# Reordering one pass of a graph layer: where the one-hots of slots 0 and 1, the turn of block A and the request for x stand

## The chip, the core and the metric

The kernel runs on one core of a Trainium2 chip. The engines of the core work side by side, each through its own list of instructions in order, and wait for one another by semaphores: TensorE (PE, with its weight loads shown as PEld), VectorE (DVE), ScalarE (ACT), GpSimd (POOL) and SyncE (SP), which here only issues transfers. The metric is the device time of one execution in microseconds; lower is better. The time before the change is 260.56 us, the median of three runs from 260.49 to 260.68 us.

## The reference

There are 12500 nodes with 128 numbers each (x) and 412500 directed edges with 48 numbers each, sorted by their receiver `dst`. What is computed is

```
h   = relu(layernorm(x))                       # per node, 128 numbers
agg = segment_sum(edge_attr_48, dst, 12500)    # per node, the sum of its edges' 48 numbers
u   = graph_globals[0]                         # one row for all nodes
out = x + relu([h, agg, u] @ W1 + b1) @ W2 + b2
```

W1 has 256 columns and W2 has 128. All is float32.

## The kernel before

**Tiling.** Edges come in chunks of 768; four chunks make a group, eleven groups make one pass. There are 12 passes, each over 33792 edges and 1024 nodes, and an epilogue for the rest (212 nodes). The 1024 nodes of a pass are two blocks of 512, A and B; each block has four pieces of 128 nodes. The eleven groups sit in six slots: slots 0 to 3 hold two groups each, slot 4 holds one (group 5), slot 5 holds groups 10 and 11.

**Sums over edges.** For each slot DVE builds one-hot matrices that say to which of 28 neighbouring receivers an edge belongs (`onehots`, L745, tile `oh`), PE multiplies them with the edges (`sums`, L801, into one of two PSUM banks `s`), and ACT copies the result out (L805, tile `ss`). A second set of small one-hot matrices (`places`, L751, and `places_near`, `places_far`, L764) then puts these sums at their node (`place`, L823, and `place_ends`, L785, into banks `ax` and `ay`). `place_ends` comes after all `place` and needs slot 5's copy, here called ss5, from its second matmul on.

**The nodes.** DVE takes statistics of x (`stats`, L831), a few small instructions make the variance (`variance`, L836 to L841), ACT takes the root (`root`, L845), DVE makes scale and shift (`shift`, L850 and L851), ACT normalises and applies relu piece by piece (`norm`, L857, tiles `xna` and `xnb`). PE turns the pieces (`turn`, L866), ACT copies the turned block out (L867, `hta` and `htb`), `sums_out` (L872) copies the edge sums, and the first layer is `layer_x` (L876) and `layer_e` (L881), ended by relu on ACT (L886, `hida` and `hidb`).

**The second layer runs one pass late.** `second` (L907) multiplies the hidden numbers of the pass before with W2, sixteen matmuls for block A; then DVE adds it to x + b2 and keeps it (L911, `holda`, `holdb`). For block B, three of four pieces are done early (`second_begun`, L901) and the last one later. After it DVE forms the next x + b2 (`add_b`, L861, `xba`, `xbb`), and only then may the next x be asked for: `load_x` (L597), issued by ACT for both blocks. The edge loads of L597 are issued by SP, each as soon as the sums of its slot have been taken.

**Order.** `body` writes all operations of one pass in one list; an engine's own order is the order of the list, cut down to that engine. `Flow.order` finds the waits from what each operation reads and writes. DVE, ACT and SP run the list in a hardware loop. PE runs it in blocks joined by branches: the list is cut at the operation named in `f.mark`, and the part behind the mark runs at the head of the loop. In the first pass there is no hidden layer to multiply yet, so the operations named in `f.brief` are passed over by a branch (from L301 on).

In the list of `body` before, what matters stands so: slots 0 and 1 are summed, then statistics of A, `farthest` (L692, L694), `fetch` (L730, which reads the receivers for the one-hots of the next pass), slot 2, statistics of B, variance, root, one-hots of slot 0, slot 3, shift, one piece of A normalised, slot 4, two pieces, one-hots of slot 1, slot 5, one piece, then all of B.

Of the kernel before, what the change touches and what calls it, by code (L numbers as in the profile page):

```python
# [28 lines left out]
R = 4  # L29
# [25 lines left out]
class Flow:  # L55
# [14 lines left out]
    def op(self, eng, name, reads, writes, emit, dma=False, late=None):  # L70
        self.seq.append(dict(eng=eng, name=name, r=tuple(reads), w=tuple(writes), emit=emit, dma=dma, it=self.at, late=late or {}))
# [119 lines left out]
    def run(self):  # L191
# [22 lines left out]
        def ahead(e, late=False):  # L214
            for n, c in sorted(self.ahead[e].items()):
                if (e == "PE" and n in self.weights) == late:
                    self.of[e].wait_ge(self.sem[n], (self.rank[n, c] + self.extra[n]) * self.unit(n))

        def repeat(o, i):
            waits = []  # L220
            for n, back in self.body.get(o["name"], []):
                u = self.unit(n)
                waits.append((n, self.sem[n], regs[(o["eng"], u, (self.at_lo[n] - lo - back + self.extra[n]) * u)]))
            self.emit(o, waits, i)
# [26 lines left out]
        pe = nc.tensor  # L251
        blocks = {}

        def part(name, over, come=True):

            if come:
                pe.br("pe_" + name)
            blocks[name] = nc.switch_bb("pe_" + name, parent=over and blocks[over])

        def either(under, yes, no):  # L260

            pe.br_lt(j, under, on_true="pe_" + yes, on_false="pe_" + no)

        n = 4
# [35 lines left out]
        at = "first"  # L300
        for brief, some in groupby(own[:cut], lambda o: o["name"] in self.brief):  # L301
            some = list(some)
            if not brief:
                for o in some:
                    if o["name"] in self.stops:
                        stop = "at_" + o["name"]
                        at = "go_" + o["name"]
                        above, under, to = over[stop]
                        part(stop, above)
                        either(under, to, at)  # L310
                        part(at, stop, False)
                    repeat(o, None)
                continue
            either(n + 1, "brief", "whole")
            part("brief", at, False)
            ahead("PE", True)
            for o in some:
                if o["name"] in self.sem:
                    pe.sem_inc(self.sem[o["name"]], 1)
            pe.br("pe_both")  # L320
            part("whole", at, False)
            for o in some:
                repeat(o, None)
            part("both", at)
        pe.br("pe_head")
        part("after", "gate2", False)
        self.straight(end)
# [151 lines left out]
def kernel(  # L479
# [37 lines left out]
    def bank(name):  # L517
        return psum.tile([P, BN], F32, name=name)
# [4 lines left out]
    ph = [bank("ph0"), bank("ph1")]  # L523
# [66 lines left out]
    f = Flow(nc, tc)  # L590
    op = f.op
    A, B, Z = 0, 1, 2
# [128 lines left out]
    def fetch(j):  # L721

        it = (f.at or 0) + j
        g0, g1 = it * GI + 1, min(NG, (it + 1) * GI + 1)
        m = GI * CG
        blocks = [b for b in range(NB) if b * P < g1 * CG and (b + 1) * P > g0 * CG]
        rv = rel_i.rearrange("p g (c t) -> p (g c) t", t=T)
        at = lambda i: ((i + j) * GI + 1) * CG

        op("DVE", "fr", ["relz"] + [f"rel{b}.{t0}" for b in blocks for t0 in (0, 3)], ["rel_i"], lambda i: [nc.vector.tensor_scalar(  # L730
            rv, (rel[:, :, at(i):at(i) + m] if isinstance(i, int) else rel[:, :, ds(at(i), m)]).rearrange("p t c -> p c t"),
            0.0, None, OP.add)])
# [20 lines left out]
    def onehots(s):  # L753
        g = SLOTS[s]
        onehot(s, oh[s], ["rel_i"], rel_i[:, g[0] - 1:g[0]] if len(g) == 1 else rel_i[:, g[0] - 1:g[1]:g[1] - g[0]])
# [32 lines left out]
    def keep_ends():  # L788
        op("ACT", "ssf", ["ss5"], ["ssf"], lambda i: [nc.scalar.copy(ssf, ss[5])])
# [43 lines left out]
    def variance(n, ks, m=P):  # L833
        s, v = sm[n][:m], st[n][:m]
        op("DVE", f"sm{n}.0", [f"st{k}" for k in ks], [f"sm{n}a"], lambda i: [
            nc.vector.tensor_tensor(s[:, 0:2], v[:, :, 1:3].rearrange("p r c -> p c r"), v[:, :, 4:6].rearrange("p r c -> p c r"), OP.add)])  # L836
        op("DVE", f"sm{n}.1", [f"st{k}" for k in ks], [f"sm{n}b"], lambda i: [
            nc.vector.tensor_tensor(s[:, 2], v[:, :, 1], v[:, :, 4], OP.subtract)])
        f.chain("DVE", f"sm{n}.2", [f"sm{n}a"], [f"sm{n}b"],
            lambda: nc.vector.tensor_tensor(s[:, 2], s[:, 2], s[:, 2], OP.mult),  # L840
            lambda: nc.vector.scalar_tensor_tensor(s[:, 3], s[:, 2], D / 4.0, s[:, 1], OP.mult, OP.add))  # L841

    def root(n, m=P):
        op("ACT", f"sq{n}", [f"sm{n}b", "eps"], [f"sc{n}"], lambda i: [
            nc.scalar.activation(sc[n][:m], sm[n][:m, 3], AF.Sqrt, bias=eps[:m], scale=1.0 / D)])  # L845
# [7 lines left out]
    def norm(k, some, m=P):  # L853
        n, c = k // 2, k % 2 * R
        for r in some:
            op("ACT", f"xn{k}.{r}", [f"x{k}", f"x{k}t", f"sc{n}", f"sh{n}"], [f"xn{k}"], lambda i, r=r: [
                nc.scalar.activation(xn[k][:m, r], xt[k][:m, r], AF.Relu, bias=sh[n][:m, c + r:c + r + 1], scale=sc[n][:m, c + r:c + r + 1])])  # L857
# [5 lines left out]
    def turn(k, m=P, bk=None, key="PT", eng="ACT"):  # L863
        pv = (pt if bk is None else bk)[:, :RR[k] * P].rearrange("p (r c) -> p r c", r=RR[k])
        copy = nc.scalar.copy if eng == "ACT" else nc.vector.tensor_copy
        op("PE", f"tu{k}", [f"xn{k}", "ident"], [key], lambda i: [nc.tensor.transpose(pv[:, r, :m], xn[k][:m, r], ident[:m, :m]) for r in range(RR[k])])  # L866
        op(eng, f"hT{k}", [key], [f"hT{k}"], lambda i: [copy(hT[k][:, :, :m], pv[:, :, :m])])  # L867

    def sums_out(k, m=P):
        h, r = HI * (k % 2), RR[k]  # L870
        op("ACT", f"ag{k}", [f"bk{k % 2}"], [f"ag{k}"], lambda i: [
            nc.scalar.copy(ag[k // 2][h:h + DE, :, :m], agg[k % 2][h:h + DE, :m * r].rearrange("p (c r) -> p r c", r=r))])  # L872
# [25 lines left out]
    def second_begun(k, bk, key, n):  # L898
        ov = bk.rearrange("p (r d) -> p r d", r=R)
        op("PE", f"w2{k}a", [f"hid{k}.{a}" for a in range(NH)] + ["w2"], [key], lambda i: [  # L900
            nc.tensor.matmul(ov[:, r], hid[k][:, a, r], w2[:, a], start=(a == 0), stop=(a == NH - 1)) for r in range(n) for a in range(NH)])  # L901
# [101 lines left out]
    def body(it):  # L1003
        f.at = it

        def add_slots(*some):
            for s in some:
                sums(s)
                if it < NIT - 1:
                    load_e(s, 1)  # L1010

        keep = lambda i: (i + NIT - 2) % (NIT - 1)
        add_slots(0, 1)
        stats(A)
        farthest()
        fetch(1)
        add_slots(2)
        stats(B)
        variance(0, (A, B))
        root(0)  # L1020
        onehots(0)
        add_slots(3)
        shift(0)
        norm(A, (0,))
        add_slots(4)
        norm(A, (1, 2))
        onehots(1)
        add_slots(5)
        norm(A, (3,))
        norm(B, range(R))  # L1030
        onehots(2)
        onehots(3)
        place(0, (0, 1))
        for s in (1, 2, 3, 4):
            place(s)
        place_ends((0, 1))
        second(A, P, ph[A], "PH0", keep)
        add_b(A)
        for s in (4, 5):
            onehots(s)  # L1040
        second_begun(B, ph[B], "PH1", R - 1)
        sums_out(A)
        sums_out(B)
        if it < NIT - 1:
            load_x(A, lambda i: (i + 1) % NIT * IN)
        turn(A)
        turn(B, P, po, "PO")
        second(B, P, ph[B], "PH1", keep, R - 1)
        add_b(B)
        keep_ends()  # L1050
        if it < NIT - 1:
            load_x(B, lambda i: (i + 1) % NIT * IN + BN)
        places_far()
        fetch_off(1)
        for s in (0, 1, 2, 3, 4):
            places(s)
        places_near()
        layers(layer_x)
        layers(layer_e)
        layers(relu)  # L1060
# [51 lines left out]
    f.at = NIT + 1  # L1112
    ends = [f"ot{k}" for k in range(3)] + [f"x{k}" for k in (A, B)] + [f"hold{k}.{j}" for k in (A, B) for j in range(NIT - 1)]
    op("SP", "end", [], ends, lambda i: [nc.sync.nop(nofuse=True)])
    f.mark, f.half, f.stops = "tu0", "of2", ("su1.b", "su1.c", "su2.b")
    f.brief, f.weights = ("w20", "w21a"), ("lw1h", "lw1a", "lw1b", "lw2")
    f.order((0, NIT - 1))
    tc.mark_branch_hint_location("skip", engines=[ET.PE, ET.DVE])
# [35 lines left out]
```

## Time and profile before

| what | us |
|---|---|
| median of three runs | 260.56 |
| the profiled execution, its own time | 260.67 |
| its span, first to last instruction | 258.9 |
| PE busy in the span | 238.8 |
| DVE busy | 230.8 |
| ACT busy | 127.9 |
| mean length of one pass, from pass 1 to pass 11 (second layer of A to second layer of A) | 18.07 |

The span is cut into 40 slices on the page of the profile; there the transfers are busy in almost every slice, and so are PE and DVE. With three resources nearly full, the share of busy time doesn't say which of them sets the pace. For that one has to follow, in the timeline of one pass, which instruction waits for which other, around the pass and back to the same instruction of the next one. The pass from 116.5 to 134.6 us is used for this below; times of it are counted from the start of the span.

A timeline row has the start, the duration, the engine, the line, the operation and the tiles; instructions of one form that follow each other are merged into one row with their count, and such a row's duration goes to the end of the last one. Where the engine stood idle before it, brackets say for how long and what released it.

### The profile page before, as it was taken

Reading aid. Unit: us, or ns where it says so; the run is one execution under the profiler, and the core shown is the slowest. Engines: PE = TensorE matmul, PEld = TensorE weight load, DVE = VectorE, ACT = ScalarE, POOL = GpSimd, SP = SyncE. Lnnn points to the kernel's source line nnn. Section 1 sums busy time; section 2 is a strip of 40 time slices with the busy share of each in tenths; the row PEclk is TensorE's granted clock in tenths of the full one; section 3 lists DMA queues with packets and bytes.
Section 4 is the critical chain, followed back from the end, with each engine's and each line's share of the span. In section 5 each row is a group of like instructions: output and inputs, shape, how many; then the busy total and the mean of one; then the engine's idle time right before and its main releaser. Section 6 shows DMA issues by size and latency. Waiting matters only on the chain.

```text
span 258.9 us, 17101 instructions
## 1 busy us (share of the span) xinstructions
PE 238.8 (92%) x7539; PEld 188.7 (73%) x7540; DVE 230.8 (89%) x572; ACT 127.9 (49%) x315; POOL 5.2 (2%) x18
## 2 busy tenths in 40 slices
PE   1866699899999999999999999999999999999990
PEld 1766565885976968949949869779589499598680
DVE  6699998978998998998998989989989989989740
ACT  5510273553644725725835646447257358355520
POOL 5000000000000000000000000000000000002000
PEclk9967579999999999999999999999999999999999
DMA  6999999999999999999999999999999999969951
GB/s 189 339 385 388 364 387 392 390 390 393 377 392 389 389 392 387 390 392 384 390 394 385 390 393 386 392 386 385 391 383 390 391 389 390 394 230 363 366 208 65
DMA packets 79508, 94.33 MB, mean 364 GB/s; under 512 B 3227, under 2 KB 72797, under 8 KB 79494
## 3 DMA queue, kind: packets, MB, share of 16 engines
q1 hardware_dynamic: 76086, 88.06, 95.5%
q10 hardware_dynamic: 3312, 6.03, 6.1%
q8 instruction: 7, 0.11, 0.2%
q0 software_dynamic: 96, 0.07, 0.1%
q14 instruction: 7, 0.06, 0.1%
HBM read 87.75 MB, written 6.40 MB: 364 GB/s over the span
## 4 chain that ended last, share of the span: by engine, by line
PE 78%; SPq 14%; DMA 4%; issue 1%; DVE 0%
PE s L801 23%; SPq L597 14%; PE ph L907 12%; PE ph L876 7%; PE ax L823 6%; PE ph L901 6%; PE pt L881 4%; PE pt L876 4%; DMA e<-in_edge_attr_dram 4%; PE ph L881 4%; PE po L876 4%; PE pt L866 2%; PE po L866 2%; PE ax L785 1%; PE ay L785 1%
## 5 line engine op out<-in xcount | busy, mean ns | idle before, releaser
L745 DVE TENSOR_TENSOR oh<-iota_v,rel_i 128x1344 f32<-128x1344 f32 (+1 forms) x78 | 108.7, 1435 | 0.0
L801 PEld LDWEIGHTS s<-e,oh 128*28 128x28 f32 x6336 | 74.2, 111 | 16.8 <-issue 14.5
L801 PE MATMUL s<-e,oh 128*28 128x48 f32 x6336 | 76.9, 212 | 7.4 <-issue 3.5
L886 ACT ACTIVATE hida<-pt,bias 128x512 f32<-128x512 f32 x12 | 8.2, 687 | 50.2 <-PE pt L881 50.2
L857 ACT ACTIVATE xna<-xa,shab,scab 128x128 f32<-128x128 f32 x48 | 23.7, 493 | 13.0 <-DVE shab L851 12.6
L805 ACT COPY ss<-s 128x96 f32<-128x96 f32 (+1 forms) x72 | 16.5, 229 | 26.5 <-PE s L801 25.7
L751 DVE TENSOR_SCALAR pl<-iota_w,off_i 128x186 f32<-128x186 f32 x117 | 27.6, 311 | 0.4
L907 PE MATMUL ph<-w,hida 128*128 128x128 f32 x192 | 24.6, 281 | 0.0
L857 ACT ACTIVATE xnb<-xb,shab,scab 128x128 f32<-128x128 f32 x48 | 23.5, 490 | 1.2
L907 PEld LDWEIGHTS ph<-w,hida 128*128 128x128 f32 x192 | 22.3, 191 | 0.6
L823 PE MATMUL ay<-pl,ss 128*48 128x186 f32 (+1 forms) x120 | 20.9, 324 | 0.0
L823 PE MATMUL ax<-pl,ss 128*48 128x186 f32 (+1 forms) x120 | 20.9, 324 | 0.0
L823 PEld LDWEIGHTS ax<-pl,ss 128*48 128x48 f32 x120 | 14.5, 129 | 4.1
L831 DVE BATCH_NORM_STATS2 stab<-xb 128x6 f32<-128x128 f32 x48 | 10.5, 282 | 6.9 <-DMA xb<-in_x_dram 6.9
L901 PE MATMUL ph<-w,hidb 128*128 128x128 f32 x132 | 16.5, 275 | 0.0
L901 PEld LDWEIGHTS ph<-w,hidb 128*128 128x128 f32 x132 | 15.6, 192 | 0.0
L823 PEld LDWEIGHTS ay<-pl,ss 128*48 128x48 f32 x120 | 14.5, 129 | 0.0
L876 PE MATMUL pt<-hta,w1h 128*128 128x512 f32 x24 | 13.5, 643 | 0.4 <-ACT hta L867 0.4
L881 PE MATMUL po<-ags,w1a 48*128 48x512 f32 x24 | 13.5, 641 | 0.0
L881 PE MATMUL pt<-ags,w1a 48*128 48x512 f32 x24 | 13.5, 641 | 0.0
L867 ACT COPY hta<-pt 128x512 f32<-128x512 f32 x12 | 7.0, 586 | 12.2 <-PE pt L866 12.2
L881 PE MATMUL ph<-ags,w1a 48*128 48x512 f32 x48 | 12.3, 589 | 0.0
(151 smaller groups left out, 330.3 us busy)
## 6 DMA issues: line engine op xcount, KB each, us to landing
e<-in_edge_attr_dram SPq DMA_DIRECT2D x133, 576.0 KB, 8.7
xa<-in_x_dram ACTq DMA_DIRECT2D x11, 256.0 KB, 5.4
xb<-in_x_dram ACTq DMA_DIRECT2D x11, 256.0 KB, 5.4
out_dram<-holda SPq DMA_DIRECT2D x11, 256.0 KB, 3.1
out_dram<-holdb SPq DMA_DIRECT2D x11, 256.0 KB, 3.1
holda<-in_dst_dram SPq DMA_DIRECT2D x4, 384.0 KB, 5.6
e<-in_edge_attr_dram SPq DMA_DIRECT2D x1, 720.0 KB, 4.7
xa<-in_x_dram SPq DMA_DIRECT2D x1, 256.0 KB, 6.6
```

The source lines that it names most:

```text
L597: return [f.of[eng].dma_start(dst_ap(i) if callable(dst_ap) else dst_ap, src_ap(i) if callable(src_ap) else src_ap)]
L745: op("DVE", f"oh{name}", reads + ["iota_v"], [f"oh{name}"], lambda i: [nc.vector.tensor_tensor(ov, iota_v[:, None, None, :].to_broadcast([ ...
L751: nc.vector.tensor_scalar(out[:, j], iota_w, o[j], None, OP.is_equal) for j in range(len(o))])
L801: nc.tensor.matmul(S[k][NV * c:NV * c + V, j * DE:(j + 1) * DE], o[:, (j * CG + c) * T + t], ev[:, j * CG + c, t * DE:(t + 1) * DE], start ...
L805: op("ACT", f"ss{name}", [f"S{k}"], [f"ss{name}"], lambda i: [nc.scalar.copy(sv.rearrange("p j d -> p (j d)"), S[k][:, :m * DE])])
L823: out.append(nc.tensor.matmul(agg[bk][h:h + DE, at:at + w], sv[:, j], pv[:, j, frm:frm + w], start=bk in fresh and bk not in seen, stop=Tr ...
L831: op("DVE", f"st{k}", [f"x{k}", f"x{k}t"], [f"st{k}"], lambda i: [nc.vector.bn_stats(st[k // 2][:m, c + r], xt[k][:m, r]) for r in range(R ...
L857: nc.scalar.activation(xn[k][:m, r], xt[k][:m, r], AF.Relu, bias=sh[n][:m, c + r:c + r + 1], scale=sc[n][:m, c + r:c + r + 1])])
L876: nc.tensor.matmul(o, w1h[:, a * P:(a + 1) * P], hT[k][:, :, :m], start=first, stop=False, skip_group_check=True)])
L881: nc.tensor.matmul(o, w1a[h:h + DE, a * P:(a + 1) * P], ag[k // 2][h:h + DE, :, :m], start=False, stop=True, skip_group_check=True)])
L901: nc.tensor.matmul(ov[:, r], hid[k][:, a, r], w2[:, a], start=(a == 0), stop=(a == NH - 1)) for r in range(n) for a in range(NH)])
L907: nc.tensor.matmul(ov[:m, r], hid[k][:, a, r, :m], w2[:, a], start=(a == 0), stop=(a == NH - 1)) for r in range(begun, RR[k]) for a in ran ...
```

## The change

```diff
@@ the PE list with brief operations
-            either(n + 1, "brief", "whole")
-            part("brief", at, False)
-            ahead("PE", True)
+            tag = some[0]["name"]
+            either(n + 1, "brief_" + tag, "whole_" + tag)
+            part("brief_" + tag, at, False)
+            if tag == self.brief[0]:
+                ahead("PE", True)
             for o in some:
                 if o["name"] in self.sem:
                     pe.sem_inc(self.sem[o["name"]], 1)
-            pe.br("pe_both")
-            part("whole", at, False)
+            pe.br("pe_both_" + tag)
+            part("whole_" + tag, at, False)
             for o in some:
                 repeat(o, None)
-            part("both", at)
+            part("both_" + tag, at)
+            at = "both_" + tag
@@ body
         stats(A)
         farthest()
         fetch(1)
+        onehots(0)
         add_slots(2)
         stats(B)
         variance(0, (A, B))
+        onehots(1)
+        add_slots(3)
         root(0)
-        onehots(0)
-        add_slots(3)
         shift(0)
-        norm(A, (0,))
         add_slots(4)
-        norm(A, (1, 2))
-        onehots(1)
+        norm(A, (0, 1))
         add_slots(5)
-        norm(A, (3,))
+        norm(A, (2, 3))
         norm(B, range(R))
         onehots(2)
         onehots(3)
@@ body, after place_ends, second(A), add_b(A) and the one-hots of slots 4 and 5
-        second_begun(B, ph[B], "PH1", R - 1)
         sums_out(A)
         sums_out(B)
+        turn(A)
+        second_begun(B, ph[B], "PH1", R - 1)
         if it < NIT - 1:
             load_x(A, lambda i: (i + 1) % NIT * IN)
-        turn(A)
         turn(B, P, po, "PO")
@@ the mark
-    f.mark, f.half, f.stops = "tu0", "of2", ("su1.b", "su1.c", "su2.b")
+    f.mark, f.half, f.stops = "tu1", "of2", ("su1.b", "su1.c", "su2.b")
```

On DVE the one-hots of slot 0 move from behind the variance to behind `fetch`, ahead of the statistics of B, and those of slot 1 from behind the shift to ahead of it. On ACT the root moves behind the copy of slot 3, two pieces of A (not three) are normalised ahead of slot 5's copy and two (not one) behind it, the copy of slot 4 comes ahead of all of them, and the copy of the turned A comes ahead of the request for A's next x. On PE, A is turned right behind its second layer and ahead of the begun second layer of B. The two second layers are then no longer neighbours in PE's list, so each gets its own branch, and the cut of the list moves to the turn of B. No operation is added or left out.

## The prediction

> **What bounds the kernel now.** I read the page first, then the waits of DVE, then the chain that ended last, then one pass in the timeline, engine by engine.
>
> ```profile
> span 258.9 us, 17101 instructions
> DMA  6999999999999999999999999999999999969951
> GB/s 189 339 385 388 364 387 392 390 390 393 377 392 389 389 392 387 390 392 384 390 394 385 390 393 386 392 386 385 391 383 390 391 389 390 394 230 363 366 208 65
> PE 78%; SPq 14%; DMA 4%; issue 1%; DVE 0%
> ```
>
> The transfers are busy throughout, at 384 to 394 GB/s in most slices, yet the chain of the end runs over PE for 78%. Its pieces in order of time say where PE begins to set the end:
>
> ```profile
> 39.59 10.01 DMA e<-in_edge_attr_dram
> 49.65 0.71 PE s L801 x48
> 52.24 1.98 PE ph L907 x16
> ...
> 232.90 1.98 PE ph L907 x16
> ```
>
> Until 49.65 us edges are late (passes 0 and 1). From the second layer of A in pass 1 to that in pass 11 the chain is PE's: 232.90 - 52.24 = 180.66 us for ten passes, **18.07 us a pass**. A full PE could be the bound itself, or be paced by something that it waits for a little in each pass. DVE's waits name the candidate:
>
> ```profile
> DVE stab L831 <- DMA xb<-in_x_dram: 6.9, 11, 0.8
> DVE holda L911 <- PE ph L907: 1.6, 1, 1.6
> ```
>
> DVE waits once a pass, about 0.63 us (6.9 / 11), for B's x; for PE's second layer it waited in one pass only. DVE's own pass:
>
> ```profile
> 116.48 0.87 DVE L831 BATCH_NORM_STATS2 stab<-xa 128x6 f32<-128x128 f32 x4
> ...
> 117.87 0.41 DVE L730 TENSOR_SCALAR rel_i<-rel 128x264 f32 x1
> 118.90 0.87 DVE L831 BATCH_NORM_STATS2 stab<-xb 128x6 f32<-128x128 f32 x4 [0.62 <-DMA xb<-in_x_dram]
> ...
> 120.39 1.55 DVE L745 TENSOR_TENSOR oh<-iota_v,rel_i 128x1344 f32<-128x1344 f32 x1
> 121.86 0.19 DVE L850 RECIPROCAL scab<-scab 128x8 f32<-128x8 f32 x1
> 122.09 0.17 DVE L851 SCALAR_TENSOR_TENSOR shab<-smab,scab 128x8 f32<-128x8 f32 x1
> 122.17 4.49 DVE L745 TENSOR_TENSOR oh<-iota_v,rel_i 128x1344 f32<-128x1344 f32 x3
> 126.58 0.68 DVE L911 TENSOR_TENSOR holda<-ph,xba 128x512 f32 x1
> 127.30 0.69 DVE L861 TENSOR_TENSOR xba<-xa,b_sb 128x512 f32<-128x512 f32 x1
> ...
> 130.86 0.69 DVE L861 TENSOR_TENSOR xbb<-xb,b_sb 128x512 f32<-128x512 f32 x1
> ...
> 134.55 0.86 DVE L831 BATCH_NORM_STATS2 stab<-xa 128x6 f32<-128x128 f32 x4
> ```
>
> Nothing but those 0.62 us is idle here: 134.55 - 116.48 = 18.07 us, 17.45 of work and the wait. The wait closes a loop: xbb ends at 131.55, only then is the next xb asked for, and it lands late:
>
> ```profile
> xa<-in_x_dram ACTq DMA_DIRECT2D x11, 256.0 KB, 5.4
> xb<-in_x_dram ACTq DMA_DIRECT2D x11, 256.0 KB, 5.4
> ```
>
> 131.55 + 5.4 = 136.95, 18.05 after 118.90. So xb's loop sets the pace. But there is a **second loop of the same length**, from DVE's shift over ACT and PE back to DVE:
>
> ```profile
> 121.00 0.24 ACT L805 COPY ss<-s 128x96 f32<-128x96 f32 x1 [0.19 <-PE s L801]
> ...
> 122.29 0.49 ACT L857 ACTIVATE xna<-xa,shab,scab 128x128 f32<-128x128 f32 x1 [1.05 <-DVE shab L851]
> 122.69 0.18 ACT L805 COPY ss<-s 128x48 f32<-128x48 f32 x1
> 122.82 1.02 ACT L857 ACTIVATE xna<-xa,shab,scab 128x128 f32<-128x128 f32 x2
> 123.74 0.22 ACT L805 COPY ss<-s 128x96 f32<-128x96 f32 x1
> 123.87 0.49 ACT L857 ACTIVATE xna<-xa,shab,scab 128x128 f32<-128x128 f32 x1
> ...
> 126.24 0.56 ACT L872 COPY ags<-ax 48x512 f32<-48x512 f32 x1
> 126.81 0.58 ACT L872 COPY ags<-ay 48x512 f32<-48x512 f32 x1
> 128.02 0.34 ACTq L597 DMA_DIRECT2D xa<-in_x_dram  x1
> 128.41 0.59 ACT L867 COPY hta<-pt 128x512 f32<-128x512 f32 x1 [1.01 <-PE pt L866]
> ```
>
> ```profile
> 123.90 0.28 PE L785 MATMUL ax<-plf,ssf 128*48 128x140 f32 x1
> 124.02 0.32 PE L785 MATMUL ay<-pln,ss 128*48 128x140 f32 x1
> ...
> 124.47 2.05 PE L907 MATMUL ph<-w,hida 128*128 128x128 f32 x16
> ```
>
> The shift ends at 122.26 (122.09 + 0.17). ACT normalises three pieces of A ahead of the copy of slot 5 (123.74 to 123.96). place_ends needs that copy from its second matmul on, which starts 0.06 behind it, at 124.02. The second layer of A follows at 124.47 and ends at 126.52; holda starts at 126.58. DVE came to holda at that same moment, behind the one-hots, so no wait is shown, but the room is 0.06 us at most.
>
> **The change part by part.**
>
> *Slot 0's one-hots ahead of B's statistics.* They fill the place of the wait: xbb still ends 4.97 behind holda's start (131.55 - 126.58), so xb lands 4.97 + 5.4 = 10.4 behind it. The statistics of B now come 7.97 (134.55 - 126.58) + 1.80 (116.48 to fetch's end at 118.28) + 0.04 + 1.47 = 11.28 behind holda. **-0.62 us** for xb's loop; 0.9 us of room, and if an x load grew by more than that the wait would be back. 1.47 is the place of one one-hot (120.39 to 121.86, also 4.41 / 3 from 122.17 to 126.58). The 0.04 is the step between two DVE instructions of which the second needs the first (reciprocal's end 122.05 to 122.09): the one-hots now stand right behind fetch, whose result they read.
>
> The Trainium skill, "VectorE: DVE Perf Modes", section "The DRAIN you can't avoid", says that a DVE instruction doesn't start before the pipeline of the one ahead has emptied, and that a semaphore between them cost nothing extra. By that the 0.04 is nothing, 0.4 us less in ten passes. The rows differ both ways: unlinked one-hots start 1.47 apart though each takes 1.55, linked ones leave 0.04.
>
> *Slot 1's one-hots ahead of the shift.* On DVE they only change places, 1.47 us either way, but the shift and all of ACT's normalisation now stand behind them. They do cover the root (before, slot 0's did that). From holda to the shift's end, before: 7.97 + 1.80 + 0.62 + 1.49 (118.90 to 120.39, statistics and variance) + 1.47 + 0.40 = 13.75. After: 7.97 + 1.80 + 0.04 + 1.47 + 1.49 + 1.47 + 0.40 = 14.64. **+0.89 us.** The root behind slot 3's copy costs nothing: that copy starts 4.5 us into DVE's pass (121.00 - 116.48), the shift then 6.3 into it (1.80 + 0.04 + 1.47 + 1.49 + 1.47), and the root takes 0.3.
>
> *Two pieces, not three, ahead of slot 5's copy.* From the shift's end to the copy's start, before 123.74 - 122.26 = 1.48; after, 0.03 to the first piece and 0.92 for two (122.82 to 123.74) = 0.95. **-0.53 us.** The copy of slot 4 moves out of the way for nothing, between root and shift.
>
> *The rest of that loop* stays: copy to second layer 0.73 (123.74 to 124.47), second layer to holda 2.11 (124.47 to 126.58). Sum before: 13.75 + 1.48 + 0.73 + 2.11 = **18.07**, the pass measured. After: 14.64 + 0.95 + 0.73 + 2.11 = **18.43**. DVE's own work would take it to holda 0.9 us earlier (17.45 + 0.04 = 17.49 us a pass), but there it now waits for the second layer, which waits for ss5, which waits for the shift. What goes as a wait for xb comes back, larger, as a wait for PE.
>
> *A turned early, its copy ahead of asking for xa.* In the row above, A's copy starts 0.04 behind the request (128.02 + 0.34), which had waited for xba (127.99). Now it can't be held there. But behind ss5 there is one piece more (about 0.5), so sums_out starts 3.0 behind ss5's start instead of 2.50, the two copies take 1.14, and hta is copied from 4.2 to 4.8 behind ss5 instead of 4.67 to 5.26. A gain of some 0.5 in hta, of which PE can use little (its first layer starts at 129.04, 0.04 behind the end of hta, and about when the four matmuls ahead of it were through), and on a stretch that now ends in a wait for ss5: **nothing**. The request for xa follows at 4.7 instead of 4.28 behind ss5 and lands 5.4 later, 10.1; A's next statistics come at 2.84 + 7.97 = 10.8. It is hidden by 0.7 us; without that cover DVE would wait for xa. SP's queue of edge loads isn't passed by anything.
>
> *The second branch on PE.*
>
> ```profile
> 126.36 1.50 PE L901 MATMUL ph<-w,hidb 128*128 128x128 f32 x12
> ...
> 127.70 0.60 PE L866 MATMUL pt<-ident,xna 128*128 128x128 f32 x4
> ...
> 129.04 1.13 PE L876 MATMUL pt<-hta,w1h 128*128 128x512 f32 x2
> ```
>
> No row prices it alone. Bounds: nothing, since the cut of the list, with the loop's own branches, lies between the first two of these rows, and the turn starts before the twelve matmuls end (127.86); and 0.45 us, the whole stretch from place_ends' gated matmul to the second layer, which has a branch already. I take nothing, from the nearer rows; the new branch also lies behind the second layer of A, outside the loop of 18.43.
>
> **The sum.** +0.36 us a pass, ten passes behind pass 1's second layer: +3.6 us. Passes 0 and 1 wait for edges, and the epilogue behind 232.90 is the same list. The profiled execution took 260.67 us, 0.11 above the median of 260.56: 264.3 by the one, **264.2 us** on the scale of the median.
>
> **The rivals.**
>
> *Faster: the change does what it seems meant to.* The place is holda. If DVE, running ahead, doesn't meet the second layer of A there, because slot 5's copy is made as soon as slot 5 is summed and not behind two pieces, the loop of 18.43 is open. Then PE binds, whose only gaps in the rows above are 0.12 ahead of the gated matmul and less for hta: about 17.9 us a pass. The transfers allow hardly more: eleven edge loads of 576 KB and two of 256 KB are 7.01 MB a pass, at the 394 GB/s of the best slice 17.8 us. At 17.95 ten passes give back 1.2 us: 259.4. It decides from the point where the shift ends 0.36 us earlier than I reckon. For it: the wait that is removed is the only one DVE has in each pass. Against it: ACT works in order, and the copy stands behind the pieces in the list. Chance 0.08.
>
> *Same: one of the two loops has more room than one pass shows*, and +0.36 shrinks below 0.05 a pass. Against it: the second sum before hits 18.07 exactly. 260.1 to 261.1; chance 0.05.
>
> *Slower still: the loop of 18.43 and something more*, xa landing behind A's statistics, or the new branch exposed. Another 0.1 to 0.2 a pass would give 265.2 to 266.2. Chance 0.12.
>
> *Much slower: PE's new wait lowers its clock.*
>
> ```profile
> PEclk9967579999999999999999999999999999999999
> ```
>
> In the third to sixth slices, where PE waits for edges, the granted clock falls to between 0.5 and 0.7. Were half a microsecond a pass enough for that, a second layer, the turns and the first layer (some 10 us of PE a pass) could take up to twice as long, 100 us more. Against it: the clock holds at 0.9 or more over all passes that have PE's small gaps, and PE would still be busy for 97% of a pass. Chance 0.01.
>
> The Trainium skill, "TensorE: Matmul & The Clock Gate", section "Part 1: The HAM clock gate (the \"warmup\" mystery)", puts the idle time after which the clock is halved at about 3.4 us. By that rule this case falls away.
>
> **How the numbers follow.** The forecast has 0.74. Its terms are read to 0.01 us, about ten of them, and ten passes multiply an error: 0.1 a pass is 1 us, 263.2 to 265.2. To take in part of the slower case the range goes to 265.4, and down to 262.6 for a loop shorter by 0.16. A measurement of this kernel tells about 0.2% (0.5 us) from no change. Faster 0.08, within 0.2% 0.05, slower 0.87.
>
> **What the changed profile would show.** If right: DVE's wait for xb is gone (6.9 us to under 1), and a new one of holda for PE's L907 stands at about 0.9 us a pass, 9 us in ten; the second layers of A lie 18.4 apart; ss5 starts 0.95 behind the shift's end; place_ends shows a gap of about half a microsecond ahead of its second matmul; hta waits for nothing; the rate falls to about 381 GB/s; SP waits longer for PE. If holda shows no wait and the pass is below 18.0, the loop is wrong. If the pass is above 18.5, the branch or xa is the place to look.

## The result, and the profile after

The changed kernel took 264.2 us (median of four runs, 263.59 to 264.65) against 260.62 us before (four runs, 260.49 to 261.26): **1.3% slower**, ratio 1.0131, 95% interval 1.0102 to 1.016. The profiled execution took 263.89 us, 3.2 us more than the one before (260.67). One execution of all, of the version below with the root moved alone, took 399.3 us at a granted clock of 0.579 and is left out of that version's ratio.

From the page of the changed kernel, the span, the rate of the transfers in 40 slices, and the chain that ended last by engine:

```profile
span 262.0 us, 17127 instructions
GB/s 199 346 389 386 363 387 392 391 390 386 389 392 389 390 392 376 385 392 369 390 394 362 390 380 372 392 372 386 392 363 388 392 365 390 394 189 373 365 186 64
DVE 50%; PE 18%; SPq 14%; issue 7%; ACT 4%; DMA 4%; DVEq 1%
```

The chain has moved from PE (78%) to DVE (50%), and from the sixteenth slice on the rate dips to 362 to 380 in every second or third slice, where before it held 383 to 394. Its pieces in order of time (start, duration, what) give the length of a pass:

```profile
51.89 2.00 PE ph L910 x16
...
236.05 1.98 PE ph L910 x16
```

(236.05 - 51.89) / 10 = **18.42 us a pass** against 18.07. Ten passes cost 3.5 us more; pass 1 happened to begin its second layer 0.35 us earlier (51.89, not 52.24), and 3.15 remain. DVE's waits (what waited for what, us in total, times, longest):

```profile
DVE holda L914 <- PE ph L910: 9.8, 11, 1.4
...
DVE stab L834 <- DMA xa<-in_x_dram: 0.5, 1, 0.5
```

The wait for xb, 6.9 us in 11 passes, isn't in the list any more. In its place holda waits 9.8 us for the second layer. One pass of DVE in the timeline of the changed kernel:

```profile
117.12 0.86 DVE L834 BATCH_NORM_STATS2 stab<-xa 128x6 f32<-128x128 f32 x4
...
118.51 0.41 DVE L733 TENSOR_SCALAR rel_i<-rel 128x264 f32 x1
118.95 1.56 DVE L748 TENSOR_TENSOR oh<-iota_v,rel_i 128x1344 f32<-128x1344 f32 x1
120.43 0.86 DVE L834 BATCH_NORM_STATS2 stab<-xb 128x6 f32<-128x128 f32 x4
...
121.92 1.55 DVE L748 TENSOR_TENSOR oh<-iota_v,rel_i 128x1344 f32<-128x1344 f32 x1
123.39 0.20 DVE L853 RECIPROCAL scab<-scab 128x8 f32<-128x8 f32 x1
123.62 0.17 DVE L854 SCALAR_TENSOR_TENSOR shab<-smab,scab 128x8 f32<-128x8 f32 x1
...
127.57 0.69 DVE L914 TENSOR_TENSOR holda<-ph,xba 128x512 f32 x1 [0.84 <-PE ph L910]
...
135.54 0.87 DVE L834 BATCH_NORM_STATS2 stab<-xa 128x6 f32<-128x128 f32 x4
```

ACT and PE in the same pass:

```profile
122.25 0.18 ACT L808 COPY ss<-s 128x48 f32<-128x48 f32 x1
123.83 1.02 ACT L860 ACTIVATE xna<-xa,shab,scab 128x128 f32<-128x128 f32 x2 [1.40 <-DVE shab L854]
124.75 0.22 ACT L808 COPY ss<-s 128x96 f32<-128x96 f32 x1
...
128.94 0.59 ACT L870 COPY hta<-pt 128x512 f32<-128x512 f32 x1
129.01 0.35 ACTq L600 DMA_DIRECT2D xa<-in_x_dram  x1
```

```profile
124.37 0.40 PE L788 MATMUL ax<-plf,ssf 128*48 128x140 f32 x2
125.02 0.32 PE L788 MATMUL ay<-pln,ss 128*48 128x140 f32 x1 [0.25 <-ACT ss L808]
...
125.48 2.05 PE L910 MATMUL ph<-w,hida 128*128 128x128 f32 x16
```

Read it backwards from holda. It starts at 127.57, when the second layer (125.48) is through. That layer stands behind place_ends, whose gated matmul starts 0.65 us behind the first (124.37 to 125.02; 0.12 before the change): PE waits for slot 5's copy. The copy starts at 124.75, behind two pieces of A, and these behind the shift, which ends at 123.79 and not earlier because slot 1's one-hots stand ahead of it. DVE then stands still 0.84 us.

### The profile page after: what moved, and what is told of

The parts are those of the page before. It is cut to its first block, busy times and chain, and to the rows that moved or that the text cites. A ratio compares the mean times of both kernels' runs of the same rounds, so it can differ in the third digit from the quotient of the medians.

```text
span 262.0 us, 17127 instructions
## 1 busy us (share of the span) xinstructions
PE 241.2 (92%) x7539; PEld 189.1 (72%) x7540; DVE 231.8 (88%) x572; ACT 129.7 (50%) x315; POOL 5.0 (2%) x18
## 4 chain that ended last, share of the span: by engine, by line
DVE 50%; PE 18%; SPq 14%; issue 7%; ACT 4%; DMA 4%; DVEq 1%
DVE oh L748 20%; SPq L600 14%; PE ph L910 10%; DVE pl L754 7%; DVE stab L834 6%; DMA e<-in_edge_attr_dram 4%; ACT xna L860 4%; DVE holda L914 3%; DVE holdb L914 2%; PE ay L788 2%; DVE plf L767 2%; DVE rel_i L733 2%; DVE pln L767 1%; DVE far L695 1%; DVE smab L839 1%
## 5 line engine op out<-in xcount | busy, mean ns | idle before, releaser
L914 DVE TENSOR_TENSOR holda<-ph,xba 128x512 f32 x12 | 8.3, 691 | 9.8 <-PE ph L910 9.8
L879 PE MATMUL pt<-hta,w1h 128*128 128x512 f32 x24 | 12.4, 598 | 0.0
L879 PE MATMUL po<-htb,w1h 128*128 128x512 f32 x24 | 12.3, 592 | 0.0
```

Of the source, the lines that this page charges most:

```text
L879: nc.tensor.matmul(o, w1h[:, a * P:(a + 1) * P], hT[k][:, :, :m], start=first, stop=False, skip_group_check=True)])
L914: op("DVE", f"ho{k}", [key, f"xb{k}"] + (["spare"] if k == A else []), [f"hold{k}.{keep(f.at)}"], lambda i: [nc.vector.tensor_tensor(cols( ...
```

## The experiments

**The theory.** The pass is set by the loop holda, DVE up to the shift, pieces of A, slot 5's copy (ss5), second layer of A, holda. **Rival 1**: all normalising is late, so the turn and the first layer are; how many pieces stand ahead of ss5 is no matter. **Rival 2**: the second branch and the early turn cost PE.

| kernel | us (median) | ratio to before, 95% interval | us a pass |
|---|---|---|---|
| no piece of A ahead of ss5 | 259.63 | 0.9947 (0.9923 to 0.9972) | 17.93 |
| one piece | 259.59 | 0.9948 (0.9931 to 0.9965) | 17.94 |
| two pieces (the changed kernel) | 264.2 | 1.0131 (1.0102 to 1.016) | 18.42 |
| three pieces | 269.51 | 1.0326 (1.0261 to 1.0392) | 18.94 |
| moves of the one-hots without the turn | 264.47 | 1.0138 (1.0073 to 1.0202) | 18.41 |
| the turn alone | 261.24 | 1.0025 (0.9997 to 1.0053) | 18.07 |
| slot 0's move without slot 1's | 259.5 | 0.9955 (0.9939 to 0.9972) | 17.94 |
| slot 1's without slot 0's | 269.29 | 1.0331 (1.0308 to 1.0354) | 18.94 |
| before, slot 0's one-hots moved | 264.57 | 1.0156 (1.0116 to 1.0196) | 18.49 |
| before, the root moved | 260.44 | 0.9982 (0.9964 to 1.0) | 18.05 |
| before, both of these moved | 259.36 | 0.9938 (0.9913 to 0.9962) | 17.94 |
| no piece, slot 4 not loaded anew | 269.18 | 1.0328 (1.0305 to 1.0351) | 17.91 |
| no piece, a quarter of slot 4 loaded | 258.92 | 0.9931 (0.9906 to 0.9955) | 17.90 |

A pass is the distance of the second layers of A in pass 1 and pass 11 on the chain, divided by ten.

### Pieces ahead of slot 5's copy: none, one, three

Three edits of the changed kernel, in one cut:

```diff
         add_slots(4)
-        norm(A, (0, 1))
+        # none: nothing    one: norm(A, (0,))    three: norm(A, (0, 1, 2))
         add_slots(5)
-        norm(A, (2, 3))
+        # none: norm(A, range(R))    one: norm(A, (1, 2, 3))    three: norm(A, (3,))
```

> As the changed kernel, but no piece of A is normalised ahead of slot 5's copy (all four behind it). Theory (the loop shift, two pieces, slot 5's copy, second layer of A, holda sets the pass of 18.42 us): the copy no longer waits for the shift, that loop is open, holda hardly waits; the next bound is some 17.95 us a pass (transfers, and the way over the turned A to the first layer, which I work out as 14.64 + 5.85 + 5.51 + 7.74 + 2.11 = 35.85 us for two passes). Ten passes at -0.47: about 259.5 us, faster than both kernels. Rival 1 (the loss is that all normalising comes later, so turn and first layer are late): the number of pieces ahead of the copy does not matter, 264.2 or, since one copy stands ahead of them, 264 to 265. Rival 2 (the second branch and the early turn cost PE): 264.2.

> As the changed kernel, but three pieces of A ahead of slot 5's copy, as before the change. Theory: 0.53 us more from the shift's end to that copy, pass 18.42 + 0.53 = 18.95 us, ten passes +5.3: 269.5 us, and holda's wait for PE grows from 0.9 to about 1.4 us a pass. Rival 1 and rival 2: 264.2, since neither the shift nor the branches move.

> As the changed kernel, but one piece of A ahead of slot 5's copy. Theory: the loop is 14.64 + 0.43 + 0.73 + 2.11 = 17.91 us, just under the 17.93 us that the pass took with no piece ahead, so that one binds: 259.6 us, 259.2 to 260.0. With none 17.93, one 17.93, two 18.42, three 18.94 the line has its bend between one and two pieces. Rival (each piece ahead costs its half a microsecond from none on): 262.

DVE's waits, first with none, then with three:

```profile
DVE holda L914 <- PE ph L910: 4.3, 11, 0.7
```

```profile
DVE holda L914 <- PE ph L910: 16.0, 11, 2.3
```

Neither the one-hots nor the branches move here, and the time goes from 259.6 over 264.2 to 269.5 us, with the bend between one and two pieces where the sum puts it (0.43 instead of 0.95 from shift to copy). From two to three pieces a pass grows by 0.52, one piece on ACT. Both rivals fall as the cause: with none and with three pieces they had 264.2, at most 265. holda still waits 0.4 us a pass with none (4.3 / 11): there DVE is ahead of PE and nothing behind it is late.

### The turn, and the moves of the one-hots, each alone

```diff
-        sums_out(A)
-        sums_out(B)
-        turn(A)
         second_begun(B, ph[B], "PH1", R - 1)
+        sums_out(A)
+        sums_out(B)
         if it < NIT - 1:
             load_x(A, lambda i: (i + 1) % NIT * IN)
+        turn(A)
...
-    f.mark, f.half, f.stops = "tu1", ...
+    f.mark, f.half, f.stops = "tu0", ...
```

> The moves of the one-hots with the order on ACT up to the second layer of A; the turn of A, its copy and the request for x stand as before the change, and the two second layers are neighbours again with one branch. Theory: nothing of the turn lies on the loop: 264.2 us, 263.9 to 264.6, pass 18.42. Rival 2 (branch and early turn cost PE): 259.5 to 260.6.

The kernel with the turn alone keeps the lines with a minus and has the one-hots, root and pieces of the kernel before.

> The kernel before with only the early turn of A, its copy ahead of the request for x, and the second branch. Theory: the loops of 18.07 us stay, xb's wait of some 0.6 us a pass stays: 260.6 us, within 0.3 of before. Were the 0.05 to 0.1 us that PE waits for hta worth something: 259.6 to 260. Rival 2: 263 to 264.2.

The moves of the one-hots, with the order on ACT that goes with them, bring the whole loss without the turn, 18.41 us a pass. The turn alone leaves the pass at 18.07 and xb's wait in place (7.0 us in 11 passes). Its ratio has 1 within the interval: no gain, and no cost that these ten runs could tell.

### Slot 0's move and slot 1's, each without the other

```diff
 without slot 1's:                     without slot 0's:
         variance(0, (A, B))                    fetch(1)
-        onehots(1)                    -        onehots(0)
         add_slots(3)                           add_slots(2)
...                                    ...
         norm(A, (0, 1))                        variance(0, (A, B))
+        onehots(1)                    +        onehots(0)
         add_slots(5)                           onehots(1)
```

> As the changed kernel, but slot 1's one-hots again behind the shift and slot 5's copy on the list; two pieces of A stay ahead of that copy. Theory: from holda to the shift's end 14.64 - 1.47 = 13.17 us and some 0.45 us of waiting for the root, which nothing covers now; loop 13.6 + 0.95 + 0.73 + 2.11 = 17.4 us, open; DVE's own pass 17.49 + 0.45 = 17.94 and the transfers' 17.93 bind: 259.6 us, 259.2 to 260.0, DVE waiting for ACT's root 0.4 to 0.5 us a pass instead of for xb or PE. Rival (the whole reordering, not slot 1's place, costs): 262 to 264.2.

> As the changed kernel, but slot 0's one-hots back behind the variance, so that both slots' stand between variance and shift. Theory: the wait for xb is back (0.6 us a pass) and the shift is late as well: from holda to the shift's end 10.43 + 1.49 + 1.47 + 1.47 + 0.40 = 15.26 us, loop 15.26 + 0.95 + 0.73 + 2.11 = 19.05 us a pass, ten passes +6.3 over the changed kernel: 270.5 us, 269.8 to 271.2. Rival (the waits for xb and for PE are alternatives, DVE does not pay both): 264 to 266.

Slot 0's move without slot 1's is faster than both kernels; DVE's list of waits there begins with the root, 4.4 us in 12. Slot 1's alone pays twice, for xb and for PE:

```profile
DVE holda L914 <- PE ph L910: 9.6, 11, 1.2
DVE stab L834 <- DMA xb<-in_x_dram: 6.2, 11, 0.7
```

It came out 0.5 us under the range given (269.8 to 271.2): 18.94 us a pass and not 19.05. The wait for xb is 0.56 us a pass (6.2 / 11) where I had 0.66, for xb lands 5.3 us behind its request and not 5.4.

### Is one moved line enough?

From the kernel before:

```diff
         fetch(1)
+        onehots(0)
         add_slots(2)
         stats(B)
         variance(0, (A, B))
         root(0)
-        onehots(0)
         add_slots(3)
```

> The kernel before with one line moved: slot 0's one-hots stand behind fetch, ahead of slot 2 and B's statistics; all else (three pieces of A ahead of slot 5's copy, the turn, one branch) as before. Theory: the wait for xb goes; from holda to the shift's end 7.97 + 1.80 + 0.04 + 1.47 + 1.49 + 0.4 for the root, uncovered + 0.40 = 13.57 us, loop 13.57 + 1.48 + 0.73 + 2.11 = 17.89, under the transfers' 17.94, which bind: 259.5 us, 259.1 to 259.9, some 0.4% faster than before. Were the turn's part of the change needed for that gain: 260.0 to 260.5.

A miss: 264.57, slower, with 18.49 us a pass. The timeline of this kernel, ACT and then PE:

```profile
140.73 0.30 ACT L845 ACTIVATE scab<-smab,eps 128x8 f32<-128x8 f32 x1 [1.23 <-DVE smab L841]
140.94 0.22 ACT L805 COPY ss<-s 128x96 f32<-128x96 f32 x1
```

```profile
138.80 1.94 PE L801 MATMUL s<-e,oh 128*28 128x48 f32 x164
141.21 1.22 PE L801 MATMUL s<-e,oh 128*28 128x48 f32 x96 [0.47 <-ACT ss L805]
```

With slot 0's one-hots early the variance is ready 0.9 us later in DVE's pass, so the root is, and slot 3's copy stands behind the root on ACT. Slots 3 and 5 share one PSUM bank, so slot 5's sums (the 96 matmuls) can't begin before that copy: 141.21, just behind the copy's end at 141.16. That is another loop of the same kind, variance, root, slot 3's copy, slot 5's sums, second layer, holda. The next kernel moves the root as the change does:

```diff
-        root(0)
         add_slots(3)
+        root(0)
```

> The kernel before with two lines moved: slot 0's one-hots behind fetch, and the root behind slot 3's sums and their copy. Theory (what the one-line version lost came from slot 3's copy standing behind the root on ACT, which waits for the variance, while slot 5's sums wait for that copy's bank): PE's wait of 0.63 us a pass ahead of slot 5's sums is gone, the pass falls from 18.49 to the transfers' 17.94, 259.5 us, 259.1 to 259.9, faster than before and level with the other versions that give up slot 1's move. Rival (three pieces of A ahead of slot 5's copy are too many once slot 0's one-hots stand early): 262 to 264.6, with the wait at slot 5's copy and not ahead of its sums.

> The kernel before with only the root moved behind slot 3's copy, the one-hots as before. Theory: the root is covered by slot 0's one-hots either way and xb's loop of 18.07 us stays, wait for xb 0.6 us a pass: 260.5 us, within 0.4 of before. Rival (the root's place alone gains what the two-line version gains): 259.5.

Both came as expected: 259.36 us with both lines moved, 260.44 with the root alone. So the root's move inside the change is not for show: slot 0's early one-hots need it. These two moved lines are the smallest version found that beats both kernels, **0.62% faster than before** (ratio 0.9938, 0.9913 to 0.9962).

### What binds at 17.93 to 17.94 us

Four orders stop at the same pass. In the profile of the two-line version the rate is level in all passes behind the fourteenth slice:

```profile
GB/s 189 339 385 387 366 387 392 390 390 393 386 391 392 390 392 391 390 391 391 390 394 389 390 392 389 391 389 390 391 391 391 391 391 390 394 250 318 367 275 65
```

7.01 MB in 17.94 us are 391 GB/s, so the transfers can be what is left. For the version with no piece ahead of ss5 there was a second candidate, a loop over two passes, from holda to the shift, four pieces of A and four of B, sums_out, hta, the first layer, the next second layer and holda. Its sum is 35.85 us for two passes. To part them, loads of edges are left out; the sums of slot 4 then use edges of the first pass in their place, so that these two kernels serve for their times alone:

```diff
-                if it < NIT - 1:
+                if it < NIT - 1 and s != 4:
                     load_e(s, 1)
```

> As the kernel with no piece ahead of slot 5's copy, but slot 4's group of edges is not loaded anew in the passes (its sums use the first pass's edges): 576 KB of 7.01 MB a pass less. If the transfers alone set the 17.93 us: a pass falls to PE's own 17.75 or so, ten passes -1.8, some 257.8 us or less since edges are also late in the first passes. If the way from the shift over the turned A to the first layer (35.85 us in two passes, 17.93 a pass) sets it: the pass stays at 17.9, and only the first passes gain, about 258 to 259 us; PE then waits for hta each pass and no longer for edges.

The total missed by 10 us, and the pass did not: 17.91. The loss is all at the start (second layer of pass 1 at 62.35, not 52.42): PE's first sums begin at 29.89 us, where they began at 16.48. A load that isn't in the loop any more seems to be waited for ahead of the loop, in front of everything. The next kernel therefore keeps the load and its wait and cuts it to one chunk of four:

```diff
+            m = 1 if s == 4 and (f.at or 0) >= 0 else CG
-            dma(..., e[s][:, k * CG:(k + 1) * CG], ... GE ...)
+            dma(..., e[s][:, k * CG:k * CG + m], ... m * CE ...)
```

> As the kernel with no piece ahead of slot 5's copy, but in the passes only one of the four chunks of slot 4's group is loaded anew (432 KB a pass less; the sums of the other three use the first pass's edges). The load keeps its place and its wait inside the loop. Theory: the late start of the kernel that left the whole load out (second layer of pass 1 at 62.3 us, not 52.4) came from the wait for that load standing ahead of the whole loop, and is gone here; the passes are again 17.73 and 18.08 in turn, mean 17.91, by the loop over two passes: second layer of pass 1 at 51 to 52.5 us, 258.5 to 259.5 us in all. Rival (leaving out part of the transfers itself delays the start or costs time): 262 or more.

The start is back at 51.74 us, as it should be if that wait was the cause; the total is 258.92, and the pass 17.90. Its chain lists the second layer only in every other pass:

```profile
51.74 2.00 PE ph L911 x16
87.53 2.00 PE ph L911 x16
...
230.74 1.98 PE ph L911 x16
```

35.79 us for two passes against the 35.85 worked out. ACT and PE tell why passes differ:

```profile
73.53 0.58 ACT L871 COPY hta<-pt 128x512 f32<-128x512 f32 x1
...
91.26 0.58 ACT L871 COPY hta<-pt 128x512 f32<-128x512 f32 x1
```

```profile
74.17 1.13 PE L880 MATMUL pt<-hta,w1h 128*128 128x512 f32 x2
...
92.01 1.02 PE L880 MATMUL pt<-hta,w1h 128*128 128x512 f32 x2
```

In one pass the first layer starts 0.06 us behind hta's end (74.11), in the next 0.17 behind it (91.84): it waits in every other pass. So with nothing ahead of ss5, transfers and this loop lie 0.03 us apart. In the versions that leave slot 1's one-hots behind the shift that loop is 1.5 us shorter by the sum.

No run took edges away from the other three orders, but the traces show PE waiting for edges in all four. The last load of a pass brings the second half of slot 5's edges. In passes 1 to 11 of the two-line version, of the one with slot 0's move alone and of the one with one piece, and in nine of these eleven passes with none, the first matmul on this half starts 0.04 us after the load has landed. It then stands some 0.08 us behind the matmul ahead of it, 0.22 with slot 0's move alone, against 0.02 where the edges are there. With a quarter of slot 4 loaded, the edges are there 1.5 to 2.6 us early in every pass. In the kernel before, the load lands 0.19 us ahead of that matmul in pass 3 and 1.11 us ahead in pass 11, 0.115 us more each pass. Left alone the transfers would go at about 18.07 - 0.12 = 17.95 us a pass, an estimate that meets the four orders.

## Why the prediction was right, step by step

| step of the loop | predicted | measured, from the rows above |
|---|---|---|
| holda to A's next statistics | 7.97 | 7.97 (127.57 to 135.54) |
| A's statistics to fetch's end | 1.80 | 1.80 (117.12 to 118.92) |
| gap to slot 0's one-hots | 0.04 | 0.03 |
| slot 0's one-hots | 1.47 | 1.48 (118.95 to 120.43) |
| B's statistics and variance | 1.49 | 1.49 (to 121.92) |
| slot 1's one-hots | 1.47 | 1.47 (to 123.39) |
| shift | 0.40 | 0.40 (to 123.79) |
| shift to ss5 | 0.95 | 0.96 (to 124.75) |
| ss5 to second layer | 0.73 | 0.73 (to 125.48) |
| second layer to holda | 2.11 | 2.09 (to 127.57) |
| a pass | 18.43 | 18.42 |

**What bounds the kernel now** held in the main: xb's loop set the pace, and a second loop, closed by ss5, stood close behind it. The first opened as forecast (xb's wait gone), the second took over, with 0.89 us a pass in holda where 0.9 was forecast. That only the second counts is shown by the pieces, which change nothing else.

**One sum proves less than the prediction makes of it.** The 13.75 us of the second loop before contain DVE's 0.62 us of waiting for xb. A walk over all rows of a pass, waits included, gives the length of the pass whatever binds. That it came to 18.07 is therefore no sign of a second loop of the same length, nor an argument against the rival of no change. Without that wait the loop has 17.45 us of its own. What the forecast rests on is that each link was tight before (ACT idle 1.05 us for the shift, the gated matmul 0.06 behind ss5, holda 0.06 behind the second layer) and that the sum after, 18.43, has no wait in it. The change took the loop from 17.45 to 18.43: 1.47 for slot 1's one-hots and 0.04 for the gap, less 0.53 for the piece.

**Luck.** The pass is what was forecast; that the median of the total came out at 264.2 to the tenth is in part chance. The four runs lie 1.1 us apart, and pass 1's second layer began between 51.74 and 52.91 us in the profiles here, the one at 62.35 aside.

**The gap behind fetch.** The Trainium skill, "VectorE: DVE Perf Modes", section "The DRAIN you can't avoid", would have the semaphore there cost nothing; the row shows 0.03 us of gap, the linked step that the rows of before showed, near enough to make no odds at 0.3 us in ten passes.

**The turn** was costed at nothing, and alone it brought nothing. One detail was off: the request for xa was to follow the end of A's copy, 4.7 us behind ss5. It went out at 129.01, 4.26 behind ss5 and 0.07 after the copy began. It cost nothing either way.

**The second branch** was taken as nothing between bounds of 0 and 0.45 us: the pass with it (18.42) and without it (18.41) are alike.

**The clock**, the rival with a chance of 0.01: place_ends' gap grew by 0.53 us a pass, and the granted clock stayed at nine tenths or more from the seventh slice to the last but one:

```profile
PEclk9977569999999999999999999999999999999997
```

That agrees with the rule of the Trainium skill, "TensorE: Matmul & The Clock Gate", section "Part 1: The HAM clock gate (the "warmup" mystery)", which asks for some 3.4 us of idle time.

**The faster rival** named the right place: with ss5 no longer behind two pieces the kernel takes 259.6 us, for which 259.4 was forecast.

**What I hadn't seen**: that slot 5's sums hang on slot 3's copy, and with it on the root. The prediction asked only whether the root's new place costs anything, and it doesn't; the one-line version shows what the old place costs beside slot 0's early one-hots.

## What to carry to other kernels

When engines are all nearly full, write down each loop that comes back to the same instruction one pass later, add up its rows without the waits for what lies outside it, and compare the sums: here xb's loop had 18.07 us and the other 17.45, and an order that opens the first and takes the second to 18.43 gave the loss to 0.01 us a pass. Filling a wait with work that stands ahead of something others wait for only moves the wait; fill it with work that no loop waits for, and check what shares an in-order engine (a copy behind a root, a copy behind two pieces). Where two things arrive together (holda, 0.06 us) the profile shows no wait, and yet whichever is made later sets the pace at once.

## What the runs showed of the hardware beyond that

A transfer request that stands behind a copy in ACT's list started while the copy ran (129.01, the copy from 128.94 to 129.53), whereas a copy behind a request waited until it had been issued (before: 128.02 + 0.34, copy at 128.41, and 0.04 us behind the request in every pass but the first; the profile puts this wait down to PE's turn, which had ended 0.11 us earlier). And x loads of 256 KB took 5.3 us to land with three pieces, where a pass had 18.94 us for its 7.01 MB, and 5.4 to 5.5 in the two-line version, where it had 17.94.
